# A selective scan on one core: which engine makes the products with B, how far ahead, and when a block's output is written back

## The chip, the cores and the metric

The kernel runs on one core of a Trainium2 chip. The metric is the device time of one execution in microseconds (us). A core has five engines that run at the same time, each with its own queue of instructions in a fixed order: TensorE (PE in the profile, its weight loads PEld), VectorE (DVE), ScalarE (ACT), GpSimd (POOL) and SyncE (SP), which here issues the DMA transfers. Engines wait for one another by semaphores. SBUF is the working memory, PSUM holds the results of TensorE.

## The reference

The program is a chain of four layers on an input of 2 x 128 x 64 x 64 fp32. Layers 0 to 2 are untouched. The change is in layer 3, a state-space layer: the normalised image is scanned in four directions, each scan is a Mamba block with 256 inner channels and 16 states per channel, and the four outputs are fused and added to the input.

```python
xz = x @ W_in.T
xh, z = jnp.split(xz, 2, axis=-1)
...
xh = jax.nn.silu(xc).transpose(0, 2, 1)          # xc: causal convolution of 4 taps
x_dbl = xh @ W_xp.T                               # -> dt, Bm, Cm
dt = jax.nn.softplus(dt @ W_dt.T + b_dt)
A = -jnp.exp(A_log)
dA = jnp.exp(dt[..., None] * A)                   # the decays
dBu = dt[..., None] * Bm[:, :, None, :] * xh[..., None]   # the products with B
def step(h, inp):
    dA_t, dBu_t = inp
    h = dA_t * h + dBu_t
    return (h, h)
_, hs = lax.scan(step, h0, (dA.transpose(1, 0, 2, 3), dBu.transpose(1, 0, 2, 3)))
y = jnp.einsum('lbdn,bln->bld', hs, Cm)           # multiplication with C, sum over states
y = y + xh * Dp
y = y * jax.nn.silu(z)
return y @ W_out.T
```

## The kernel before

**Tiling.** Layer 3 works through 64 blocks: 2 images, 4 directions, 8 blocks of 512 positions each. The 256 inner channels are two halves (`hf` 0 and 1) of 128. The 16 states are four groups of four (`ng` 0 to 3). A *group* is one (block, `hf`, `ng`): 128 channels by 4 states by 512 positions, so a block has eight groups, in the order `hf` 0 with `ng` 0 to 3, then `hf` 1 with `ng` 0 to 3. The 512 rows of a group are laid out as four *quarters* of 128 partitions (32 channels by 4 states), so that a group's tile `db` is 128 x 4 x 512.

**What happens to a group k.** `weights(k)` (L1384) spreads B over the partitions by a matmul into the PSUM tile `pbc` (pool `psb`, two buffers). `db_dve(k)` (L1400) multiplies it on VectorE with the spread input, for the first n quarters, into `db`; `db_pool(k)` (L1408) does the other 4 - n on GpSimd, from a copy `b4` of B that DMAs have spread over the partitions (`copies`, L1391)[...]. `expo` (L1417) makes the decays of one quarter on ScalarE into a PSUM tile `da` (three buffers). `scan` (L1423) is the recurrence of one quarter on VectorE; it overwrites `db`. `keep` (L1431, ScalarE) copies the last state for the next block, `cmul` (L1436, GpSimd) multiplies the whole `db` with C in place, and `sums` (L1441, TensorE) adds up the states into the PSUM tile `py`. After that the `db` buffer is free again; the pool `l3wk` has four. The table `ND[hf][ng]` (L1130) is n, the quarters that VectorE makes.

**What happens once a block.** `gate` (VectorE) multiplies with silu(z); `project` (L1458, TensorE) adds the projection to the image so far; `finish` (L1468, ScalarE) copies this PSUM tile back into the image, or in the last direction to the output. The next block is prepared at the same time: `conv`, `xproj`, `delta`, `sum_parts` and others (TensorE), silu, softplus and copies (ScalarE), `spread` (L1364, GpSimd), and a round trip through DRAM that spreads the inputs over partitions (`spread_store`, `spread_load` on SP).

**What sets the order.** Every engine's queue is written out by hand under `manual_schedule`. The main loop (L1600) goes over k, one group at a time; `slot` is k modulo 8. In the turn of group k it issues: the transfers of this slot; `weights(k + 2)`; `finish` of the block before where slot is 6; then for each quarter q an `expo` two quarters ahead and the `scan` of (k, q), with `keep(k - 1)` after the first `expo` and a `gate` after q = 1 in slots 2 and 6; then `db_dve(k + 1)`, `db_pool(k + 1)`, `cmul(k - 1)`, the preparation of the next block for this slot (`front_pe`, `front_act`, `front_pool`: two `spread` in slots 3 and 4, softplus in slots 1 and 2, silu with its table loads in slots 4 and 7), and `sums(k - 2)`. In slot 5 `sums(k - 2)` comes first and is followed by `project` and the next block's first `conv`. `psm`, the PSUM pool that `project` and the convolutions share, has two buffers. In eight blocks (22 to 29 of the loop's count) the layer norm of the second image is done beside the rest: `ln_mean`, `ln_less` after the scans of slot 0, `ln_var` and `ln_log` in slot 3, `ln_root`, `ln_scale` (GpSimd, slot 4).

The lines of the loop around the change:

```python
                if slot == 6 and 1 <= i <= NBK:
                    finish(i - 1)
                for q in range(4):
                    ...
                    if 4 * k + q + AHEAD < len(units):
                        expo(*units[4 * k + q + AHEAD])
                    ...
                    if live:
                        scan(k, q)
                ...
                if more:
                    db_dve(k + 1)
                    db_pool(k + 1)
                if ended:
                    cmul(k - 1)
```

Of the kernel before, what the change touches and what calls it, by code (L numbers as in the profile page):

```python
# [10 lines left out]
F32 = mybir.dt.float32  # L11
# [1109 lines left out]
def layer3(g, I, out):  # L1121
# [5 lines left out]
    nc, tc = g.nc, g.tc  # L1127
    NJ = 4

    ND = ((4, 2, 1, 4), (1, 4, 1, 4))  # L1130
    NNG = N_STATE // NJ
    HB = 1
    HC = 3
    with ExitStack() as ctx:
# [39 lines left out]
                    nc.tensor.transpose(pw[:, s * P : (s + 1) * P], ws, g.ident)  # L1174
                nc.vector.tensor_copy(wcs[:, hf].rearrange("p s o -> p (s o)"), pw)
        d4 = ctx.enter_context(tc.tile_pool(name="l3d4", bufs=2))
        wk = ctx.enter_context(tc.tile_pool(name="l3wk", bufs=4))
        up = ctx.enter_context(tc.tile_pool(name="l3u", bufs=2))
        ck = ctx.enter_context(tc.tile_pool(name="l3ck", bufs=2))

# [203 lines left out]
        def weights(k):  # L1384

            i, hf, ng = groups[k]
            pb = psb.tile([P, BLK], F32, name="pbc")
            nc.tensor.matmul(pb, sel[:, ng].rearrange("p j c -> p (j c)"), S[i]["bc"], start=True, stop=True)  # L1388
            G[k] = {"pb": pb}

        def copies(i, x, ng):  # L1391

            if x == "b" and ND[0][ng] == ND[1][ng] == 4:
                return
            t = S[i][x, ng] = ck.tile([P, BLK], F32, name=f"{x}4_{ng}", bufs=1)
            r0 = NJ * ng + (N_STATE if x == "c" else 0)
            for j in range(NJ):
                nc.sync.dma_start(t[32 * j : 32 * j + 32], S[i]["bx"][r0 + j].partition_broadcast(32))

        def db_dve(k):  # L1400
            i, hf, ng = groups[k]
            x, n = G[k], ND[hf][ng]
            x["db"] = wk.tile([P, 4, BLK], F32, name="db")
            nc.vector.tensor_tensor(  # L1404
                x["db"][:, :n, :], x.pop("pb").unsqueeze(1).to_broadcast([P, n, BLK]), S[i]["d4", hf][:, 1, :n, :], ALU.mult
            )

        def db_pool(k):  # L1408
            i, hf, ng = groups[k]
            x, n = G[k], ND[hf][ng]  # L1410
            if n == 4:
                return
            nc.gpsimd.tensor_tensor(  # L1413
                x["db"][:, n:, :], S[i]["b", ng].unsqueeze(1).to_broadcast([P, 4 - n, BLK]), S[i]["d4", hf][:, 1, n:, :], ALU.mult
            )

        def expo(k, q):  # L1417
            i, hf, ng = groups[k]
# [17 lines left out]
        def cmul(k):  # L1436
            i, hf, ng = groups[k]
            v = G[k]["db"]
            nc.gpsimd.tensor_mul(v, v, S[i]["c", ng].unsqueeze(1).to_broadcast([P, 4, BLK]))  # L1439
# [28 lines left out]
        def finish(i):  # L1468
            b, nd, c = blocks[i]
            s_ = S.pop(i)  # L1470
            if nd == 0:
                nc.scalar.activation(s_["xv"], img(s_["pf"]), AF.Identity, bias=vec(g, "b_fuse"))
            elif nd < 3:
                nc.scalar.copy(s_["xv"], img(s_["pf"]))
            else:
                res = ck.tile([P, BLK], F32, name="res", bufs=1)
                nc.scalar.copy(res, s_["pf"])
                nc.sync.dma_start(out[b, :, c * BLK : (c + 1) * BLK], res)
# [29 lines left out]
        def transfers(i, slot):  # L1508
            if i < NBK:
                if slot == 1:  # L1510
                    bc_store(i)
                elif slot == 4:
                    spread_store(i, 0)
                elif slot == 5:
                    spread_load(i, 0)
                    spread_store(i, 1)
            if slot == 0 and i - 1 < NBK:
                spread_load(i - 1, 1)
            for x, ahead in (("b", 3), ("c", 1)):
                j, ng = divmod(8 * (i - 1) + slot + ahead, 8)  # L1520
                if ng < NNG and 0 < j < NBK:
                    copies(j, x, ng)
# [32 lines left out]
        with tc.manual_schedule():  # L1555
            tc.keep_in_program_order(nc.scalar.preload_act_table_set("natural_log_exp_and_others"))
            nc.scalar.activation(am, am, AF.Exp)
            nc.vector.tensor_scalar(am, am, -1.0, None, ALU.mult)
            nc.vector.memset(xt[:, :HC], 0.0)
            nc.vector.memset(xt[:, HC + L :], 0.0)  # L1560
            nc.vector.memset(xn[:, HB - 1, HW - HC :], 0.0)
            nc.vector.memset(xn[:, HB + HW, :HC], 0.0)

            for t in range(NBLK + 2):
                slot = t - 2
                if slot == 6:
                    for k in range(2):
                        weights(k)
                    db_dve(0)
                    db_pool(0)  # L1570
                if slot >= 0:
                    front_pe(0, slot)
                    front_act(0, slot)
                    front_pool(0, slot)
                if slot == 1:
                    bc_store(0)
                elif slot in (3, 4):
                    spread_store(0, slot - 3)
                    if slot == 3:
                        spread_load(0, 0)  # L1580
                        copies(0, "b", 0)
                        copies(0, "c", 0)
                if t < NBLK:
                    for part in (ln_mean, ln_less, ln_square):
                        part(0, t)
                if 0 <= t - 1 < NBLK:
                    for part in (ln_var, ln_log, ln_root, ln_scale, ln_store):
                        part(0, t - 1)
                if t == 1:
                    begin(0)  # L1590
                    conv(0, 1)
                    conv_silu(0)
            for ng in range(1, NNG):
                copies(0, "b", ng)
                copies(0, "c", ng)
            units = [(k, q) for k in range(len(groups)) for q in range(4)]
            AHEAD = 2
            for u in range(AHEAD):
                expo(*units[u])
            for k in range(len(groups) + 7):  # L1600
                i, slot = divmod(k, 8)
                live = k < len(groups)
                more = k + 1 < len(groups)
                ended = 1 <= k <= len(groups)
                transfers(i + 1, slot)
                if k + 2 < len(groups):
                    weights(k + 2)
                norm = next_norm(i)
                if slot == 6 and 1 <= i <= NBK:
                    finish(i - 1)  # L1610
                for q in range(4):
                    if norm and slot == 3 and q == 3:
                        ln_log(*norm)
                    if 4 * k + q + AHEAD < len(units):
                        expo(*units[4 * k + q + AHEAD])
                    if norm and q == 0:
                        if slot == 0:
                            ln_mean(*norm)
                        elif slot == 3:
                            ln_var(*norm)  # L1620
                    if q == 0 and ended:
                        keep(k - 1)
                    if live:
                        scan(k, q)

                    for j, hf in (((k - 6) // 8, 0), ((k - 10) // 8, 1)):
                        if q == 1 and 8 * j + 6 + 4 * hf == k and 0 <= j < NBK:
                            gate(j, hf)
                if norm and slot == 0:
                    ln_less(*norm)  # L1630
                if more:
                    db_dve(k + 1)
                    db_pool(k + 1)
                if ended:
                    cmul(k - 1)

                if slot == 5 and 0 <= k - 2 < len(groups):
                    sums(k - 2)
                if slot == 5 and 1 <= i <= NBK:
                    project(i - 1)  # L1640
                front_pe(i + 1, slot)
                front_act(i + 1, slot)
                front_pool(i + 1, slot)
                if norm:
                    if slot == 1:
                        ln_square(*norm)
                    elif slot == 3:
                        ln_root(*norm)
                    elif slot == 4:
                        ln_scale(*norm)  # L1650
                    elif slot == 6:
                        ln_store(*norm)
                if live:

                    if slot == 6 and i % (4 * NBLK) < NBLK // 2:
                        for n in range(2):
                            turn(blocks[i][0], 2 * (i % (4 * NBLK)) + n)

                if slot != 5 and 0 <= k - 2 < len(groups):
                    sums(k - 2)  # L1660
# [160 lines left out]
```

## Time and profile before

| | us |
|---|---|
| median of 3 runs | 5898.72 (5897.96 to 5899.47) |
| profiled execution, its time | 5899.89 |
| profiled execution, its span | 5898.1 |
| layer 3's scans, first to last in the trace | 2523 to 5884 |
| busy in the whole span: DVE, POOL | 4452.2, 3632.0 |
| busy in the whole span: PE, ACT | 4930.2, 3816.1 |

The profile's page gives, for the whole span, how long each engine was busy, the same in 40 equal slices with a digit for tenths, and the costliest groups of instructions: line, engine, operation, the tile written and the tiles read, their shapes, the count, the busy time and the mean duration in ns, and behind the last bar the idle time of the engine just before these instructions with what ended it. The layers 0 to 2 take the first 2450 us; shares over the whole span therefore say little on layer 3, and the views are best asked for its stretch alone. A timeline line has the start, the time, the engine, the line and operation, the tiles, the count of merged instructions, and in brackets an idle time ahead of it with the instruction that ended it. A waits line has who waited for whom, the total, the number of times and the longest.

### The profile page before, as it was taken

Reading aid. Unit: us, or ns where it says so; the run is one execution under the profiler, and the core shown is the slowest. Engines: PE = TensorE matmul, PEld = TensorE weight load, DVE = VectorE, ACT = ScalarE, POOL = GpSimd, SP = SyncE. Lnnn points to the kernel's source line nnn. Section 1 sums busy time; section 2 is a strip of 40 time slices with the busy share of each in tenths; the row PEclk is TensorE's granted clock in tenths of the full one; section 3 lists DMA queues with packets and bytes.
Section 4 is the critical chain, followed back from the end, with each engine's and each line's share of the span. In section 5 each row is a group of like instructions: output and inputs, shape, how many; then the busy total and the mean of one; then the engine's idle time right before and its main releaser. Section 6 shows DMA issues by size and latency. Waiting matters only on the chain.

```text
span 5898.1 us, 58825 instructions
## 1 busy us (share of the span) xinstructions
PE 4930.2 (84%) x19238; PEld 1735.4 (29%) x19238; DVE 4452.2 (75%) x4266; ACT 3816.1 (65%) x5499; POOL 3632.0 (62%) x1200
## 2 busy tenths in 40 slices
PE   7999999989978779877777787878777787777776
PEld 3333333334434334322222222222222222222221
DVE  5333333355124688589999999999999999999998
ACT  4888888840035511377777777777777777777775
POOL 5111111100010021089999999999999999999999
PEclk8999999999988889988888888888888888888887
DMA  5000001030056200056655556555655566555564
GB/s 155 19 19 19 19 19 33 1 59 1 4 112 109 64 11 0 20 131 146 143 133 135 130 140 145 128 131 141 151 134 134 129 139 146 139 132 134 137 148 104
DMA packets 345402, 558.75 MB, mean 95 GB/s; under 512 B 70480, under 2 KB 125280, under 8 KB 344000
## 3 DMA queue, kind: packets, MB, share of 16 engines
q1 hardware_dynamic: 341952, 551.37, 40.4%
q10 hardware_dynamic: 3136, 3.56, 0.2%
q8 instruction: 152, 2.49, 0.2%
q14 instruction: 162, 1.33, 0.1%
HBM read 465.59 MB, written 89.13 MB: 94 GB/s over the span
## 4 chain that ended last, share of the span: by engine, by line
PE 52%; DVE 27%; POOL 9%; issue 5%; DMA 4%; ACT 2%; SPq 1%; DVEq 0%; POOLq 0%; ACTq 0%
DVE db L1429 18%; PE ps L287 10%; PE acc L303 8%; DVE db L1404 7%; POOL db L1439 6%; PE pm L1294 6%; PE m L1052 6%; PE m L566 5%; PE py L1447 2%; PE pm L1359 2%; PE pm L1466 2%; PE pm L1464 2%; PE acd L812 2%; DMA dx<-dd 1%; POOL dd L1367 1%
## 5 line engine op out<-in xcount | busy, mean ns | idle before, releaser
L1439 POOL TENSOR_TENSOR db<-db,c 128x2048 f32<-128x2048 f32 x512 | 2313.4, 4535 | 92.3 <-ACT hl L1434 82.6
L1429 DVE TENSOR_TENSOR_SCAN db<-da,hl,db 128x512 f32<-128x512 f32 x1792 | 2166.1, 1266 | 69.1 <-ACT da L1420 21.1
L1420 ACT ACTIVATE da<-dd,am 128x512 f32<-128x512 f32 x2048 | 1398.0, 689 | 727.5 <-DVE db L1429 701.2
L293 ACT ACTIVATE e<-ps 128x1024 f16<-128x1024 f32 x1024 | 992.2, 1021 | 135.6 <-PE ps L287 123.9
L1388 PE MATMUL pbc<-bc,sel 64*128 64x512 f32 x512 | 288.3, 563 | 695.4 <-DVE db L1404 695.3
L1413 POOL TENSOR_TENSOR db<-b,dd 128x1536 f32<-128x1536 f32 (+1 forms) x256 | 811.5, 3170 | 9.0 <-PE py L1447 4.4
L1404 DVE TENSOR_TENSOR db<-pbc,dd 128x2048 f32<-128x2048 f32 (+2 forms) x512 | 785.3, 1534 | 0.6 <-PE pbc L1388 0.6
L314 DVE RECIPROCAL rec<-acc 32x512 f32<-32x512 f32 x64 | 214.9, 3358 | 640.4 <-PE acc L303 640.4
L321 POOL TENSOR_TENSOR parts<-parts 32x512 f32<-32x512 f32 x64 | 80.5, 1257 | 976.2 <-DVE parts L320 976.2
L1447 PE MATMUL py<-db,fold 128*32 128x512 f32 x4096 | 639.7, 701 | 39.8 <-POOL db L1439 38.4
L287 PE MATMUL ps<-q,k 32*128 32x512 f32 x4096 | 656.4, 643 | 3.6 <-DVE flag L250 2.8
L303 PE MATMUL acc<-e,v 128*128 128x512 f16 x2048 | 532.1, 382 | 0.0
L1388 PEld LDWEIGHTS pbc<-bc,sel 64*128 64x128 f32 x512 | 105.8, 207 | 1184.1 <-DVE db L1404 1070.4
L1052 PE MATMUL m<-v,u 128*128 128x512 f32 x864 | 379.7, 603 | 49.3 <-DVE v L1021 49.3
L1359 PE MATMUL pm<-dd,ident 128*128 128x512 f32 x512 | 365.3, 852 | 4.6 <-ACT dd L1352 4.4
L1429 DVE TENSOR_TENSOR_SCAN db<-da,db 128x512 f32<-128x512 f32 x256 | 294.8, 1206 | 30.4 <-ACT da L1420 22.5
L303 PEld LDWEIGHTS <-v 128*128 128x128 bf16 x2048 | 158.5, 97 | 510.6 <-issue 389.4
L287 PEld LDWEIGHTS ps<-q,k 32*128 32x128 f32 x4096 | 229.4, 184 | 228.4 <-issue 169.6
L566 PE MATMUL m<-comb,w 64*128 64x512 f32 (+4 forms) x1296 | 269.9, 575 | 0.0
L686 POOL TENSOR_SCALAR yt<-y 32x512 f32<-32x512 f32 x8 | 18.2, 2272 | 379.8 <-DVE y L677 379.4
L1052 PEld LDWEIGHTS m<-v,u 128*128 128x128 f32 x864 | 166.9, 194 | 262.1 <-issue 216.1
L1294 PE MATMUL pm<-xn,wcs 128*128 128x512 f32 x512 | 237.1, 606 | 3.0 <-ACT z L1312 2.6
(317 smaller groups left out, 5991.2 us busy)
## 6 DMA issues: line engine op xcount, KB each, us to landing
dd<-dx SPq DMA_DIRECT2D x1024, 256.0 KB, 6.8
dx<-dd SPq DMA_DIRECT2D x128, 512.0 KB, 3.3
c<-bx SPq DMA_DIRECT2D x1024, 64.0 KB, 2.2
b<-bx SPq DMA_DIRECT2D x768, 64.0 KB, 3.3
hats<-pos SPq DMA_DIRECT2D x136, 256.0 KB, 9.8
q<-qd SPq DMA_DIRECT2D x32, 512.0 KB, 7.5
w<-in_conv0T SPq DMA_DIRECT2D x18, 288.0 KB, 8.8
q<-in_x SPq DMA_DIRECT2D x8, 512.0 KB, 6.3
```

The lines of the kernel that those rows point to most:

```text
L287: nc.tensor.matmul(ps[:, i, :], k4[h % 2][rows, kb // 4, :], q4[h % 2][rows, qb * BLK : (qb + 1) * BLK], start=True, stop=True,)
L293: nc.scalar.activation(e[:, :n, :], ps[:, :n, :], AF.Exp)
L303: nc.tensor.matmul(acc, v3[b][:, kb, h, :], e[:, i, :], start=(kb == 0), stop=(kb == NS - 1))
L566: yield lambda q=q, dy=dy, src=src, i0=i0, i1=i1: nc.tensor.matmul(m[:, i0 * NF : i1 * NF], w[half, dy, q, x, :], src, start=(dy == KC and ...
L1052: nc.tensor.matmul(m[x], weights[j][:, dy, x, :], v[j][b][:, x, r0 : r0 + RP, :].rearrange("p r i -> p (r i)"), start=(dy == 0), stop=(dy ...
L1294: nc.tensor.matmul(pu, wcs[:, hf, s, :], window(blk, sgn * s), start=(s == 0), stop=(s == 3))
L1404: nc.vector.tensor_tensor(x["db"][:, :n, :], x.pop("pb").unsqueeze(1).to_broadcast([P, n, BLK]), S[i]["d4", hf][:, 1, :n, :], ALU.mult)
L1413: nc.gpsimd.tensor_tensor(x["db"][:, n:, :], S[i]["b", ng].unsqueeze(1).to_broadcast([P, 4 - n, BLK]), S[i]["d4", hf][:, 1, n:, :], ALU.mult)
L1420: nc.scalar.activation(da, S[i]["d4", hf][:, 0, q, :], AF.Exp, scale=am[:, hf, q, ng : ng + 1])
L1429: nc.vector.tensor_tensor_scan(d1, d0, d1, 0.0 if first else hl[:, hf, ng, q, :], ALU.mult, ALU.add)
L1439: nc.gpsimd.tensor_mul(v, v, S[i]["c", ng].unsqueeze(1).to_broadcast([P, 4, BLK]))
L1447: nc.tensor.matmul(S[i]["y", hf][32 * q : 32 * q + 32, :], fold, G[k]["db"][:, q, :], start=False, stop=(ng == NNG - 1),)
```

## The change

It alters which engine makes which products, the time at which GpSimd makes them, the number of `db` buffers, and the place of `finish`:

- `ND` changes from ((4, 2, 1, 4), (1, 4, 1, 4)) to ((4, 0, 1, 4), (4, 4, 0, 4)). VectorE still makes 21 of a block's 32 quarters. GpSimd makes all four quarters of two groups (`hf` 0 `ng` 1, `hf` 1 `ng` 2) and three of a third (`hf` 0 `ng` 2). Groups with n = 0 get no matmul in `weights` and no VectorE product; for `ng` 0 no copy of B is loaded any more.
- `db_pool` is called two groups ahead (for k + 2, after `cmul(k - 1)`) instead of one (for k + 1, before `cmul(k - 1)`); the copies of B start one group earlier; the pool `l3wk` has five buffers.
- `finish` of the block before moves within the turn of slot 6 from ahead of all four `expo` to ahead of the last.

```diff
-    ND = ((4, 2, 1, 4), (1, 4, 1, 4))
+    ND = ((4, 0, 1, 4), (4, 4, 0, 4))
...
-        wk = ctx.enter_context(tc.tile_pool(name="l3wk", bufs=4))
+        wk = ctx.enter_context(tc.tile_pool(name="l3wk", bufs=5))
...
         def weights(k):
             i, hf, ng = groups[k]
+            G[k] = {}
+            if ND[hf][ng] == 0:
+                return
             pb = psb.tile([P, BLK], F32, name="pbc")
             nc.tensor.matmul(pb, sel[:, ng].rearrange("p j c -> p (j c)"), S[i]["bc"], start=True, stop=True)
-            G[k] = {"pb": pb}
+            G[k]["pb"] = pb
...
+        def db_tile(k):
+            if "db" not in G[k]:
+                G[k]["db"] = wk.tile([P, 4, BLK], F32, name="db")
+            return G[k]["db"]
...
         def db_dve(k):
             i, hf, ng = groups[k]
-            x, n = G[k], ND[hf][ng]
-            x["db"] = wk.tile([P, 4, BLK], F32, name="db")
-            nc.vector.tensor_tensor(
-                x["db"][:, :n, :], x.pop("pb").unsqueeze(1).to_broadcast([P, n, BLK]), S[i]["d4", hf][:, 1, :n, :], ALU.mult
-            )
+            n = ND[hf][ng]
+            if n:
+                nc.vector.tensor_tensor(
+                    db_tile(k)[:, :n, :], G[k].pop("pb").unsqueeze(1).to_broadcast([P, n, BLK]),
+                    S[i]["d4", hf][:, 1, :n, :], ALU.mult,
+                )
...
-            for x, ahead in (("b", 3), ("c", 1)):
+            for x, ahead in (("b", 4), ("c", 1)):
...
+            db_pool(1)
             units = [(k, q) for k in range(len(groups)) for q in range(4)]
...
-                if slot == 6 and 1 <= i <= NBK:
-                    finish(i - 1)
                 for q in range(4):
+                    if slot == 6 and q == 3 and 1 <= i <= NBK:
+                        finish(i - 1)
...
                 if more:
                     db_dve(k + 1)
-                    db_pool(k + 1)
                 if ended:
                     cmul(k - 1)
+                if k + 2 < len(groups):
+                    db_pool(k + 2)
```

`db_pool` takes its tile from `db_tile` too; its arithmetic stays.

More of the change, by code (lines that the diff above doesn't have):

```diff
@@ L1398, in copies @@
                 nc.sync.dma_start(t[32 * j : 32 * j + 32], S[i]["bx"][r0 + j].partition_broadcast(32))
+        def db_tile(k):
+            if "db" not in G[k]:
+                G[k]["db"] = wk.tile([P, 4, BLK], F32, name="db")
+            return G[k]["db"]
         def db_dve(k):
             i, hf, ng = groups[k]
-            x, n = G[k], ND[hf][ng]
-            x["db"] = wk.tile([P, 4, BLK], F32, name="db")
-            nc.vector.tensor_tensor(
-                x["db"][:, :n, :], x.pop("pb").unsqueeze(1).to_broadcast([P, n, BLK]), S[i]["d4", hf][:, 1, :n, :], ALU.mult
-            )
+            n = ND[hf][ng]
[4 more added lines that the diff above has]
+                )
         def db_pool(k):
             i, hf, ng = groups[k]
[L1410 to L1415, printed above, removed]
+            n = ND[hf][ng]
+            if n < 4:
+                nc.gpsimd.tensor_tensor(
+                    db_tile(k)[:, n:, :], S[i]["b", ng].unsqueeze(1).to_broadcast([P, 4 - n, BLK]),
+                    S[i]["d4", hf][:, 1, n:, :], ALU.mult,
+                )
         def expo(k, q):
```

## The prediction

> Within one of the 64 blocks I number the eight groups 0 to 7 (0 to 3 are `hf` 0, 4 to 7 are `hf` 1) and call step s the turn of the main loop whose four scans belong to group s. "Slot" in the code is this s.
>
> **What bounds the kernel now.** First the two busy rows of the page's 40 slices, then its costliest groups.
>
> ```profile
> DVE  5333333355124688589999999999999999999998
> POOL 5111111100010021089999999999999999999999
> ...
> L1439 POOL TENSOR_TENSOR db<-db,c 128x2048 f32<-128x2048 f32 x512 | 2313.4, 4535 | 92.3 <-ACT hl L1434 82.6
> L1429 DVE TENSOR_TENSOR_SCAN db<-da,hl,db 128x512 f32<-128x512 f32 x1792 | 2166.1, 1266 | 69.1 <-ACT da L1420 21.1
> ```
>
> From about 2520 us to the end VectorE and GpSimd are both full: two engines are close to being the bound, and which one it is must be read from a single block. The groups of that stretch, shapes kept apart, give the products with B on both engines:
>
> ```profile
> L1404 DVE TENSOR_TENSOR db<-pbc,dd 128x2048 f32<-128x2048 f32 x255 | 578.1, 2267 | 0.0
> L1404 DVE TENSOR_TENSOR db<-pbc,dd 128x512 f32<-128x512 f32 x192 | 128.0, 666 | 0.0
> L1404 DVE TENSOR_TENSOR db<-pbc,dd 128x1024 f32<-128x1024 f32 x64 | 76.9, 1202 | 0.0
> ...
> L1413 POOL TENSOR_TENSOR db<-b,dd 128x1536 f32<-128x1536 f32 x192 | 660.5, 3440 | 9.0 <-PE py L1447 4.4 <-DMA c<-bx 3.0 <-POOL db L1439 0.9
> ...
> L1413 POOL TENSOR_TENSOR db<-b,dd 128x1024 f32<-128x1024 f32 x63 | 148.6, 2359 | 0.0
> ```
>
> Durations overlap or leave gaps, so the price of an instruction is read from start to start, in VectorE's timeline of a quiet block:
>
> ```profile
> 3153.59 1.20 DVE L1404 TENSOR_TENSOR db<-pbc,dd 128x1024 f32<-128x1024 f32 x1
> 3154.89 4.81 DVE L1429 TENSOR_TENSOR_SCAN db<-da,hl,db 128x512 f32<-128x512 f32 x4
> 3159.61 0.67 DVE L1404 TENSOR_TENSOR db<-pbc,dd 128x512 f32<-128x512 f32 x1
> 3160.38 2.46 DVE L1429 TENSOR_TENSOR_SCAN db<-da,hl,db 128x512 f32<-128x512 f32 x2
> ...
> 3178.29 2.27 DVE L1404 TENSOR_TENSOR db<-pbc,dd 128x2048 f32<-128x2048 f32 x1
> 3180.66 4.81 DVE L1429 TENSOR_TENSOR_SCAN db<-da,hl,db 128x512 f32<-128x512 f32 x4
> ```
>
> Four scans take 4.72 (3154.89 to 3159.61); a product of 1, 2 or 4 quarters takes 0.77, 1.30 or 2.37. A gate takes 0.58. Block: 8 x 4.72 + 4 x 2.37 + 1.30 + 3 x 0.77 + 2 x 0.58 = 52.0. The gates of quiet blocks lie 52.08 apart, so **VectorE sets the pace** there with no wait at all. GpSimd, the same way: 8 multiplications with C at 4.49, three 3.39, one 2.35, two `spread` at 1.24: 50.9. Over 64 blocks some time comes on top; the waits of VectorE (2600 to 5880 us), ScalarE and GpSimd (2523 to 5898 us), in us in total, times, longest:
>
> ```profile
> DVE db L1429 <- ACT da L1420: 33.1, 29, 3.2
> ...
> ACT xa L1474 <- PE pm L1466: 85.1, 32, 4.9
> ...
> POOL db L1439 <- ACT hl L1434: 82.6, 59, 5.7
> ```
>
> Listing every start in VectorE's timeline against its usual spacing (which also finds the short ones) puts the scans' waits in two places: before scans 2 and 3 of group 6, 23.7 us in 34 cases; before scan 3 of group 4 in the eight blocks that carry the second image's layer norm, 14.5 us. Their causes, from TensorE's and ScalarE's timelines:
>
> ```profile
> 3180.61 0.49 PE L1388 MATMUL pbc<-bc,sel 64*128 64x512 f32 x1 [3.68 <-DVE db L1404]
> ...
> 3187.08 1.12 ACT L1474 COPY xa<-pm 128x512 f32<-128x512 f32 x1 [2.06 <-PE pm L1466]
> ...
> 3755.51 0.57 ACT L1340 CAST bc<-pm 32x512 fp32r<-32x512 f32 x1 [1.59 <-PE pm L1337]
> ```
>
> In step 5 TensorE stands 3.68 us at `weights`, whose PSUM buffer VectorE frees late; `project` is queued behind it, `finish` on ScalarE waits for `project`, and the decays of group 6 are queued behind `finish`.
>
> [...] scans hold 1266 ns with GpSimd full. [...] from the trace 0.24 us (0.77 less a quarter's 0.53).
>
> **The change, part by part.**
> 1. *Products on VectorE.* The quarters stay 21 of 32, in six instructions instead of eight: 5 x 2.37 + 0.77 = 12.62 against 13.09. Saved 0.47 a block, **30 us** in 64; all of it on the path, since VectorE never idles in a quiet block. New pace 51.6.
> 2. *Products on GpSimd.* Four quarters: no such row; 3.39 + (3.39 - 2.35) = 4.43, and the equal-shaped multiplication with C takes 4.49. I take 4.45. 2 x 4.45 + 3.39 = 12.29 against 12.52: 50.7 a block. Slack 0.9.
> 3. *Order and arrival.* Moving `db_pool` behind `cmul` and one group further ahead leaves those two in the same order on GpSimd's queue; only `spread` falls one place back. I walk its queue with step 0 at 0. VectorE's steps start at 0, 4.7, 10.2, 17.9, 25.0, 32.1, 36.8, 44.5. ScalarE copies group 7's state (`keep`) behind the silu of the next block, so `cmul` 7 starts at 2.0 (read: 3150.90 against 3148.86). Product 2: 6.5 to 9.9, needed from scan 2 of group 2 on, at 11.4: 1.5 to spare. `cmul` 0 and 1 to 18.8, `cmul` 2, `spread`, `cmul` 3 to 29.4, product 6 to 33.9, needed at 36.8: 2.9 to spare. `spread` to 35.1, `cmul` 4 to 6 to 48.6, product 1 to 53.0, needed at 56.3: 3.3 to spare. So nothing on VectorE waits; cost 0, from 0 to +26 (below).
> 4. *Queues passed.* The second `spread` ends at 35.1 after step 4 begins at 25.0, about as late as now, so its store on SP too. Copies of B follow that store: eight of up to 0.9 us issue, done near 43, landed near 46, needed at 48.6 and 53. Four DMA issues a block vanish (group 0 needs no copy). Cost 0, SP being ahead.
> 5. *`weights`.* Two matmuls a block go. The one of step 5 now reuses a buffer freed in step 3, so the 3.68 goes, and the wait behind it is for `cmul` 3 (29.4). `sums` and `project` take 6 us more: 35.5, before `finish` is reached.
> 6. *`finish` later.* It reaches ScalarE at 39.9, three decays later, and ends at 41; the decay behind it still waits for a scan ending then. The 23.7 go; I leave 1: **-23**. Behind `finish` wait, on TensorE, the second convolution (its PSUM buffer) and `sums` 4: done at about 46.2. GpSimd wants the tile of `sums` 4 for product 1 at 48.6 (the fifth tile makes it this one): 2.4 to spare.
> 7. *Eight layer-norm blocks.* After step 3 VectorE now has a product of 2.37 instead of 0.77, so the wait at group 4 shrinks by 1.6 each: 14.5 to 3.7, **-11**. After step 0 it has none instead of 1.30: ScalarE's copies of the projection (3734.50, held by TensorE) let the decay of scan 3 of group 1 be ready 8.5 after the step's start, and VectorE is there at 7.7: **+7** for eight blocks (0 to +10). In other blocks that decay is ready at 6.0, needed at 7.1.
> 8. *Fifth tile, start.* The first scan waits for ScalarE (10.5 us) while GpSimd makes product 1: 0.
>
> Sum: -30 - 23 - 11 + 7 = -57 from the profiled 5899.9 (span 5898.1, 1.8 around it; the median 5898.7 is 1.2 below): 5842.
>
> **Rivals.**
> - *GpSimd paces.* It has 0.9 us in 52; if its waits for `keep` take more than that where work is due, VectorE's 0.47 returns as a wait. For: it is 98% full. Against: it is ahead at every need above. Gain of the waits alone, 34 less 3: 5869.
> - *The first quarter waits for the others.* If VectorE's quarter of group 2 is held until GpSimd's three are written (9.9 against 9.4), 0.4 x 64 = 26: 5868. Against: GpSimd now writes its share before VectorE begins, without a wait shown.
> - *Slower: the tile comes late.* `finish`, TensorE's convolution, `sums` 4, product 1, in that chain: if GpSimd stands y us a block for the tile, 0.9 are free and the rest goes to VectorE. From y = 1.8 the gain is lost; at 2.7 it is +115 - 57: 5958. It needs `sums` 4 over 4 us later than I walk it.
> - *No effect*, because waits fill every gap: 5899.
>
> **Numbers.** Likeliest case 0.70, at 5842, from 5830 (all 38 us of waits gone, none new) to 5855; GpSimd paces 0.12; first quarter 0.07; slower 0.08; none 0.03. To leave out no more than 2 in 10, the range goes from 5829 to 5874. A measurement tells about 0.2%, 12 us, from no change: faster 0.89, same 0.03, slower 0.08.
>
> **What would show it.** VectorE's products in two shapes, 5 and 1 a block; GpSimd's full ones near 4.53 us; gates 51.6 apart in quiet blocks; ScalarE's wait before L1474's copy almost gone; VectorE's waits for decays under 15 us. Wrong if VectorE waits for GpSimd's `db` in most blocks, or if GpSimd waits for `py` (tile release) for over 1 us a block.

## The result, and the profile after

The changed kernel takes 5844.64 us (median of 4 runs, 5840.38 to 5847.68) against 5899.1: a ratio of 0.9907, 95% interval 0.989 to 0.9925. The profiled execution took 5845.92 us, with a span of 5844.1. In the changed file the scans stand at L1438, VectorE's products at L1412, GpSimd's at L1421, the multiplication with C at L1448, `keep` at L1443, `finish` at L1481 to L1486.

The groups of the layer-3 stretch (2500 to 5846 us), shapes kept apart, VectorE's rows and then GpSimd's:

```profile
L1412 DVE TENSOR_TENSOR db<-pbc,dd 128x2048 f32<-128x2048 f32 x320 | 724.8, 2265 | 0.6 <-PE pbc L1391 0.6
...
L1412 DVE TENSOR_TENSOR db<-pbc,dd 128x512 f32<-128x512 f32 x64 | 42.6, 665 | 0.0
...
L1448 POOL TENSOR_TENSOR db<-db,c 128x2048 f32<-128x2048 f32 x512 | 2309.6, 4530 | 57.1 <-ACT hl L1443 52.0 <-DMA dd<-dx 3.1 <-DMA c<-bx 0.7
L1421 POOL TENSOR_TENSOR db<-b,dd 128x2048 f32<-128x2048 f32 x128 | 578.8, 4522 | 0.0
L1421 POOL TENSOR_TENSOR db<-b,dd 128x1536 f32<-128x1536 f32 x64 | 220.3, 3442 | 0.0
```

VectorE makes five full products and one of a quarter per block, and GpSimd's full product costs what a multiplication with C costs. VectorE's timeline of a quiet block:

```profile
3187.14 2.26 DVE L1412 TENSOR_TENSOR db<-pbc,dd 128x2048 f32<-128x2048 f32 x1
3189.51 9.51 DVE L1438 TENSOR_TENSOR_SCAN db<-da,hl,db 128x512 f32<-128x512 f32 x8
3198.93 0.67 DVE L1412 TENSOR_TENSOR db<-pbc,dd 128x512 f32<-128x512 f32 x1
```

Eight scans now run through without a product between them; the next product starts 9.42 after the first scan, 1.18 for each scan. Gates of quiet blocks lie 51.56 apart instead of 52.08. The waits of VectorE and GpSimd (2600 to 5830 us):

```profile
DVE db L1438 <- ACT da L1429: 11.3, 14, 1.6
DVE db L1438 <- POOL db L1421: 3.7, 5, 1.1
...
POOL db L1448 <- ACT hl L1443: 45.9, 48, 4.5
```

VectorE's 33.1 us behind decays became 11.3. In step 5 of that quiet block TensorE no longer stands at `weights`, and `finish` finds its input ready (TensorE's lines, then ScalarE's copy, which has no bracket):

```profile
3218.69 1.06 PE L1456 MATMUL py<-db,fold 128*32 128x512 f32 x8 [2.44 <-POOL db L1448]
3220.81 2.26 PE L1473 MATMUL pm<-xa,ident 128*128 128x512 f32 x2 [1.05 <-ACT z L1312]
...
3229.40 1.12 ACT L1483 COPY xa<-pm 128x512 f32<-128x512 f32 x1
```

Listing every start in VectorE's timeline as before: the waits at group 6 are gone (0.1 us); what stays is some 18 us, 15.5 of it at three places in and around the eight layer-norm blocks: 2.1 us before scan 3 of group 1, 7.3 before scan 2 of group 2, 6.1 before scan 3 of group 4. The account: 0.52 x 64 = 33 from the pace and about 22 from waits (39.8 to some 18) give 55; the spans differ by 54.0.

### The profile page after: what moved, and what is told of

It is laid out like the page before. It is cut to its first block, busy times and chain, and to the rows that moved or that the text cites. A ratio compares the mean times of both kernels' runs of the same rounds, so it can differ in the third digit from the quotient of the medians.

```text
span 5844.1 us, 57551 instructions
## 1 busy us (share of the span) xinstructions
PE 4898.7 (84%) x19110; PEld 1732.8 (30%) x19110; DVE 4430.6 (76%) x4138; ACT 3829.3 (66%) x5499; POOL 3621.2 (62%) x1136
## 4 chain that ended last, share of the span: by engine, by line
DVE 50%; PE 37%; issue 5%; POOL 3%; DMA 2%; ACT 2%; SPq 1%; DVEq 0%; POOLq 0%; ACTq 0%
DVE db L1438 36%; DVE db L1412 12%; PE ps L287 11%; PE acc L303 9%; PE m L1052 6%; PE m L566 5%; PE acd L812 2%; DVE gt L1465 1%; PE m L526 1%; POOL db L1448 1%; PE pf L775 1%; POOL db L1421 1%; PE pc L663 1%; DMA hats<-pos 1%; SPq L748 1%
## 5 line engine op out<-in xcount | busy, mean ns | idle before, releaser
L1448 POOL TENSOR_TENSOR db<-db,c 128x2048 f32<-128x2048 f32 x512 | 2309.6, 4530 | 57.1 <-ACT hl L1443 52.0
L1438 DVE TENSOR_TENSOR_SCAN db<-da,hl,db 128x512 f32<-128x512 f32 x1792 | 2155.0, 1263 | 47.6 <-ACT da L1429 9.5
L1456 PE MATMUL py<-db,fold 128*32 128x512 f32 x4096 | 618.1, 689 | 234.8 <-POOL db L1448 231.9
L1421 POOL TENSOR_TENSOR db<-b,dd 128x2048 f32<-128x2048 f32 (+1 forms) x192 | 799.1, 4162 | 0.0
L1412 DVE TENSOR_TENSOR db<-pbc,dd 128x2048 f32<-128x2048 f32 (+1 forms) x384 | 767.3, 1998 | 0.6 <-PE pbc L1391 0.6
L1391 PE MATMUL pbc<-bc,sel 64*128 64x512 f32 x384 | 209.8, 546 | 162.8 <-DVE db L1412 162.6
L1318 PE MATMUL pm<-u,wxp 128*72 128x512 f32 x256 | 197.6, 917 | 175.0 <-ACT u L1299 175.0
L1438 DVE TENSOR_TENSOR_SCAN db<-da,db 128x512 f32<-128x512 f32 x256 | 292.5, 1204 | 18.7 <-ACT da L1429 12.1
L1456 PEld LDWEIGHTS py<-db,fold 128*32 128x32 f32 x4096 | 90.4, 114 | 623.8 <-POOL db L1448 364.9
```

The lines of the kernel that those rows point to most:

```text
L1412: nc.vector.tensor_tensor(db_tile(k)[:, :n, :], G[k].pop("pb").unsqueeze(1).to_broadcast([P, n, BLK]), S[i]["d4", hf][:, 1, :n, :], ALU.mult,)
L1421: nc.gpsimd.tensor_tensor(db_tile(k)[:, n:, :], S[i]["b", ng].unsqueeze(1).to_broadcast([P, 4 - n, BLK]), S[i]["d4", hf][:, 1, n:, :], ALU ...
L1438: nc.vector.tensor_tensor_scan(d1, d0, d1, 0.0 if first else hl[:, hf, ng, q, :], ALU.mult, ALU.add)
L1456: nc.tensor.matmul(S[i]["y", hf][32 * q : 32 * q + 32, :], fold, G[k]["db"][:, q, :], start=False, stop=(ng == NNG - 1),)
```

## The experiments

Times are medians in us, ratios are to the kernel before in the same session; runs of different sessions are compared by their ratios. Lines are those of the changed kernel's numbering where nothing else is said.

### The parts alone

**The table alone** (`nd_only`): from the changed kernel, back to four tiles, B copies three ahead, no `db_pool(1)` ahead of the loop, `finish` in the old place, and

```diff
                     db_dve(k + 1)
+                    db_pool(k + 1)
                 if ended:
                     cmul(k - 1)
-                if k + 2 < len(groups):
-                    db_pool(k + 2)
```

> Only the table of products is new; GpSimd works one group ahead, four tiles, finish in its old place. Theory (the table alone is the cause): VectorE's products in six instructions, 0.47 x 64 = -30; weights of step 5 no longer holds TensorE, so project is done before finish is reached even in the old place, -20 to -23; layer-norm blocks about -1: 5842 to 5850, quiet blocks 51.6 apart. Rival (lead and fifth tile are needed): scans of the groups made whole by GpSimd wait for it, a line VectorE scan <- POOL product of over 30 us in total, 5870 to 5900.

Measured 5858.85, 0.9931 (0.9918 to 0.9945), 9 us over the theory's range. Quiet blocks are 51.6 apart and group 6's third scan never waits: the table gives the pace and takes the wait for `finish` away by itself. But group 6 has a new wait, at its first scan, 18.1 us in the eight layer-norm blocks. Its waits line, and one such place in GpSimd's and VectorE's timelines:

```profile
DVE db L1438 <- POOL db L1421: 17.4, 8, 2.5
```

```profile
3744.15 1.27 POOL L1367 TENSOR_TENSOR dd<-dd,u 128x512 f32<-128x512 f32 x1
3745.38 1.26 POOL L1243 TENSOR_TENSOR xc<-xc,sq 128x512 f32<-128x512 f32 x1
3746.61 4.53 POOL L1421 TENSOR_TENSOR db<-b,dd 128x2048 f32<-128x2048 f32 x1
...
3751.17 2.46 DVE L1438 TENSOR_TENSOR_SCAN db<-da,hl,db 128x512 f32<-128x512 f32 x2 [2.13 <-POOL db L1421]
```

Product 6 stands behind the second `spread` and `ln_scale`, 2.5 us together, and the scan waits until it ends.

**The table alone, `ln_scale` later** (`nd_scale`): in the kernel above

```diff
-                    elif slot == 4:
+                    elif slot == 5:
                         ln_scale(*norm)
```

> The kernel with only the new table of products, and ln_scale of the layer norm moved from slot 4 to slot 5 on GpSimd, behind product 6 and cmul 4. Theory (the lead of two groups matters only because it puts product 6 ahead of ln_scale and of a spread in the eight layer-norm blocks): the 18 us that VectorE waits ahead of group 6 fall to 8 or less, 5843 to 5850. Rival (the lead does something else): 5855 to 5860 as with the table alone.

5847.81, 0.9918 (0.9904 to 0.9931), within the theory's range. The wait at group 6 fell from 18.1 to 7.2. So most of what the lead of two groups brings is product 6's place on GpSimd's queue, ahead of `ln_scale`, in those eight blocks.

**`finish` alone** (`fin_only`): the kernel before with

```diff
-                if slot == 6 and 1 <= i <= NBK:
-                    finish(i - 1)
                 for q in range(4):
+                    if slot == 6 and q == 3 and 1 <= i <= NBK:
+                        finish(i - 1)
```

> Only finish moves, all else as before. Theory: the waits of group 6 (23.7 us) vanish and nothing else changes: 5874 to 5878, quiet blocks stay 52.08 apart, the waits at group 4 of the layer-norm blocks stay at 14 us. Rival (finish late holds TensorE's second convolution and with four tiles the product of VectorE): 5890 to 5910.

5881.4, 0.9969 (0.9957 to 0.998), some 5 us less gain than expected, between the two ranges. The waits at group 6 fell from 23.7 to 2.8 and those at group 4 stayed at 14.5; the span fell by 18.5.

**All but `finish`** (`fin_undone`): the changed kernel with the reverse of that diff.

> The changed kernel with finish back ahead of group 6's decays. Theory (two causes that cover each other: with step 5's weights free, project ends at about the moment finish is reached in the old place): 5843 to 5850, ScalarE waits under 30 us for project in total, VectorE under 5 us at group 6. Rival (the place of finish is what removed the 23 us): 5865 to 5870.

5848.51, 0.9914 (0.99 to 0.9927): not to be told from the changed kernel. ScalarE waits 17 us for `project` in all (9.8, 5.6 and 1.8 in its three kinds of copy), VectorE 0.2 at group 6. The new table removes the wait by itself here, the later `finish` in `fin_only`; together they don't remove it twice.

**All but the table** (`nd_old4`): the changed kernel with four tiles and

```diff
-    ND = ((4, 0, 1, 4), (4, 4, 0, 4))
+    ND = ((4, 2, 1, 4), (1, 4, 1, 4))
```

> The changed kernel with the old table of products, and four tiles[...]. Theory: VectorE is back at eight product instructions, +0.47 x 64 = 30, quiet blocks 52.08 apart; the waits at group 6 stay away because finish is late: 5872 to 5880. Rival (the earlier products of GpSimd carry the gain): 5845 to 5855.

5878.98, 0.9964 (0.995 to 0.9977), within the theory's range: quiet blocks 52.1 apart, waits at group 6 1.0 us. Without the table the pace is the old one.

**All but the fifth tile** (`four_tiles`): in the changed kernel

```diff
-        wk = ctx.enter_context(tc.tile_pool(name="l3wk", bufs=5))
+        wk = ctx.enter_context(tc.tile_pool(name="l3wk", bufs=4))
```

> The changed kernel with four tiles for the products instead of five. Theory: the tile that a product of GpSimd needs is then that of sums two groups back, still done 2 us or more before GpSimd reaches the product, so 5843 to 5848 and no wait of GpSimd for py over 5 us in total. Rival (the fifth tile carries the lead): GpSimd waits 1 us or more a block for py, quiet blocks over 52, 5870 or more.

5845.1, 0.9905 (0.989 to 0.992), within the theory's range, and no wait of GpSimd for `py`: the fifth tile is worth nothing in this kernel.

### The slower rival's chain

`finish_late`: in the changed kernel

```diff
-                    if slot == 6 and q == 3 and 1 <= i <= NBK:
+                    if (slot, q) == ((7, 1) if i < NBK else (6, 3)) and 1 <= i <= NBK:
                         finish(i - 1)
```

> The changed kernel with finish moved on by 5.9 us, to ahead of the third decay issued in step 7. It prices the slower rival's chain: finish (45.8 to 46.9), second convolution (to 50.6), sums 4 (to 52.0), product 1 (to 56.5, needed at 56.3), cmul 7 (to 61.0), product 2 (to 64.4, needed at 63.0). Theory: VectorE waits about 1.4 us a block for product 2, quiet blocks 53.0 apart, 5920 to 5945, GpSimd waits 3 us a block for py. Rival (GpSimd has room for it, or the convolution is not what holds the tile): 5845 to 5860.

5920.91, 1.0035 (1.0021 to 1.0049): slower than before the change. VectorE's waits, then GpSimd's (2600 to 5825 us):

```profile
DVE db L1438 <- POOL db L1421: 48.4, 56, 1.4
DVE db L1438 <- ACT da L1429: 29.8, 37, 2.1
...
POOL db L1421 <- issue: 53.2, 29, 4.2
POOL db L1421 <- DVE db L1412: 34.6, 15, 2.8
POOL db L1421 <- DVE db L1438: 19.2, 7, 4.0
```

By the listing VectorE waits 56.3 us in 61 blocks ahead of the second scan of group 2, 0.92 a block where 1.4 was expected, and 27.8 for the decay of group 0's third scan, which was not expected. GpSimd stands 111 us ahead of product 1 (the three lines and two smaller ones), in 53 blocks, 1.8 a block on average. The waits view names no releaser that was still busy; TensorE's and GpSimd's timelines show it:

```profile
3143.68 5.28 PE L1294 MATMUL pm<-xt,wcs 128*128 128x512 f32 x8 [3.84 <-ACT xa L1483]
3149.75 1.93 PE L1456 MATMUL py<-db,fold 128*32 128x512 f32 x16
...
3150.98 4.54 POOL L1421 TENSOR_TENSOR db<-b,dd 128x2048 f32<-128x2048 f32 x1 [1.75 <-issue]
```

The second convolution starts when `finish` ends, `sums` 4 (the first eight of the sixteen) comes behind it, and in all 53 blocks product 1 starts 0.17 us after the last matmul of `sums` 4 has ended. So the chain is the one expected. Its sizes are not. The edit moves `finish` by less than the expectation says: it stands ahead of the second decay issued in step 7, not the third, and starts (medians) 10.9 us after step 5 begins instead of 7.8, which is 3.0 later and not 5.9. `sums` 4 ends 4.6 later, because the convolution took 5.4 us there and 3.7 in the changed kernel; why is left open. The decays come late by the same chain: ScalarE's silu of the next block, which reads that convolution, waits 43.3 us for TensorE in 34 cases, and the decay of group 0's third scan is queued behind it. That the time came out at the edge of the expected range is therefore in part luck. 1.8 less the free 0.9 is close to VectorE's 0.92, but only on average: where GpSimd stands 2.7 and 1.5 in turn, VectorE waits 1.2 and 0.8.

### What the 0.24 us of an instruction is

**Two halves** (`split`): `db_dve` makes the products of `ng` 3 in two instructions.

```diff
+                for a, b in ((0, 2), (2, 4)) if ng == 3 else ((0, n),):
+                    nc.vector.tensor_tensor(
+                        db_tile(k)[:, a:b, :], pb.unsqueeze(1).to_broadcast([P, b - a, BLK]),
+                        S[i]["d4", hf][:, 1, a:b, :], ALU.mult,
+                    )
```

> The changed kernel with the four-quarter products of the two groups with ng = 3 each made in two instructions of two quarters, one behind the other: 8 product instructions a block again, same elements. Theory A (each instruction has its price of 0.24 us, wherever it stands): +0.47 x 64 = 30, 5873 to 5877. Theory B (0.19 of the 0.24 is the scan standing still until the product in front of it is written, and only 0.05 is the instruction): +0.11 x 64 = 7 or less, 5843 to 5853.

5828.45, 0.9885 (0.9869 to 0.99), below both ranges: two more instructions a block, and by the ratios some 13 us *less* than the changed kernel. Quiet blocks are 51.29 apart instead of 51.56, which is 17 us in 64. VectorE's timeline (in this file the products stand at L1414, the scans at L1440):

```profile
3202.70 2.33 DVE L1414 TENSOR_TENSOR db<-pbc,dd 128x1024 f32<-128x1024 f32 x2
3204.95 4.80 DVE L1440 TENSOR_TENSOR_SCAN db<-da,hl,db 128x512 f32<-128x512 f32 x4
```

The scan starts 80 ns before the second half ends, instead of 104 ns after a whole product: it reads the first half, which by the mean of 1204 ns for a half had ended some 1.05 us before. Theory A falls; B was right in kind and still too careful, as it left the gap standing.

**The product ahead of the last scan** (`early_product`): in the changed kernel

```diff
+                    if q == 3 and more:
+                        db_dve(k + 1)
                     if live:
                         scan(k, q)
...
-                if more:
-                    db_dve(k + 1)
```

> The changed kernel with VectorE's product for the next group issued ahead of the last scan of the group before, so that the scan behind a product does not read it. Theory B: the gap of +104 ns behind each of six products a block becomes an overlap of -83 ns as between scans, VectorE's pace falls to 51.56 - 6 x 0.187 = 50.4 and GpSimd's 50.7 becomes the bound: quiet blocks 50.7 to 51.2, 5790 to 5822. Theory A: no change, 5842 to 5849.

5805.79, 0.9845 (0.9832 to 0.9859), within Theory B's range. VectorE's timeline:

```profile
3163.23 2.26 DVE L1412 TENSOR_TENSOR db<-pbc,dd 128x2048 f32<-128x2048 f32 x1
3165.41 8.32 DVE L1438 TENSOR_TENSOR_SCAN db<-da,hl,db 128x512 f32<-128x512 f32 x7
...
3197.23 1.28 DVE L1438 TENSOR_TENSOR_SCAN db<-da,hl,db 128x512 f32<-128x512 f32 x1 [0.28 <-POOL db L1421]
```

Where the scan behind a product has nothing else to wait for, the gap is now an overlap of 79 ns. Quiet blocks are 50.7 to 50.8 apart, which is GpSimd's own sum, and VectorE waits for GpSimd in nearly every block (74 times, 40.1 us, against 5 times and 3.7): the bound has moved.

### The eight layer-norm blocks

**Layer norm later** (`norm_later`): in the changed kernel, and with `ln_var` and `ln_log` in slot 5 instead of 3 within the loop over q,

```diff
-                    if slot == 1:
+                    if slot == 2:
                         ln_square(*norm)
-                    elif slot == 3:
+                    elif slot == 5:
                         ln_root(*norm)
-                    elif slot == 4:
                         ln_scale(*norm)
```

> The changed kernel with the second image's layer norm spread otherwise: ln_square in slot 2 instead of 1, ln_var, ln_log, ln_root and ln_scale in slot 5 instead of 3 and 4. Theory: the 15 us that VectorE still waits in eight blocks come from the ScalarE and TensorE work put into steps 1 and 3, where the next product is short or TensorE's chain is long; moved to places with cover, 10 to 13 us go: 5831 to 5836. Rival (GpSimd's 1.27 more in those blocks is what makes it late): the waits stay, 5842 to 5848.

5834.84, 0.9888 (0.9872 to 0.9903), within the theory's range. GpSimd does the same work in these blocks and the waits at groups 2 and 4 are gone, so its 1.27 alone was not their cause. A wait of 6.8 us is new, before the first gate.

**With more gate buffers** (`norm_gates`): the same, with four product tiles instead of five and

```diff
-            gt = s_["gt", hf] = ck.tile([P, BLK], F32, name="gt")
+            gt = s_["gt", hf] = ck.tile([P, BLK], F32, name="gt", bufs=4)
```

> The later layer norm with four buffers for the gates' output instead of two, and four product tiles to make room. Theory (the 6.8 us that the first gate waits there are for project of the block before, which reads the buffer that this gate writes): they go, 5826 to 5830. Rival (the gate waits for its own sums): 5833 to 5837.

5836.72, 0.9898 (0.9883 to 0.9913): no gain, which is the rival's time but not for its reason. The gate's wait is gone, as the theory had it, but 8.9 us appeared before VectorE's first product of the next block, in the same eight blocks. It is the missing fifth tile: with four tiles that product takes the tile of `sums` 4, which TensorE reaches late there, and in seven of the eight blocks it starts 0.12 us after the last matmul of `sums` 4 has ended. In `norm_later`, with five tiles, it starts before `sums` 4 ends in all eight, without a wait.

**Early product and later layer norm** (`combined`): the diffs of `early_product` and `norm_later` on the changed kernel, with its five tiles.

> The early product and the later layer norm together, five tiles, two gate buffers. Theory: outside the eight layer-norm blocks GpSimd sets the pace at 50.7 as with the early product alone; in those eight GpSimd needs 51.95, so of the 53 that they take now about 1 each can go: 5795 to 5803. Rival (in those blocks TensorE's delayed project and sums become the next wait, as in the later layer norm alone): no gain over the early product, 5803 to 5810.

5797.53, 0.9827 (0.9813 to 0.9841), within the theory's range and the fastest kernel here. Its waits (2600 to 5780 us):

```profile
DVE db L1438 <- POOL db L1421: 28.2, 63, 1.3
DVE gt L1465 <- PE pm L1475: 6.4, 6, 1.5
...
POOL db L1448 <- ACT hl L1443: 2.0, 2, 1.1
```

GpSimd practically never waits: it paces layer 3.

## Why the prediction was right, point by point

The sum was -57 us and the spans differ by 54.0. That is closer than its terms are: the pace gave 33 for 30, the layer-norm blocks gained nothing (15.5 us of waits after, 14.5 before) where 4 were expected, and the two misses partly cancel. That part is luck.

1. *Products on VectorE.* The count, the sign and the price held, 0.52 a block measured for 0.47 (the rest is about 1.5 ns on each of the 32 scans); without the table (`nd_old4`) it is lost. **The reason given was wrong.** The prediction laid the saving to the count of instructions, at 0.24 us each. The traces do show a fixed part, 0.13 us in the duration (666 ns for one quarter, 533 for each further one), but 0.08 of it is hidden under the neighbour, and 0.05 is left. Most of the 0.24 is a scan that reads what the instruction in front of it has just written; 0.187 of it (104 + 83 ns) goes when the order changes. `split` adds instructions and gains. Each product that the table saved took its hand-over with it, so the price was right for this change; taken as a price per instruction it gives `split` the wrong sign and `early_product` no gain. What the 0.187 consists of, these runs don't separate.
2. *Products on GpSimd.* 4.45 start to start was taken, the timelines give 4.49; the rows give a duration of 4.522, that of the multiplication with C (4.530) less 8 ns.
3. *Order and arrival.* In quiet blocks nothing waits for GpSimd, as walked: products 2, 6 and 1 have 1.4, 3.1 and 3.2 us to spare (medians), for 1.5, 2.9 and 3.3. The walk was made for quiet blocks alone. In the layer-norm blocks product 6 has 0.3 us or less to spare in six of eight, and in and just behind them product 2 has nothing in seven cases; without the lead (`nd_only`) group 6 waits 18 us for product 6.
4. *Queues passed.* No wait on a copy of B appears on VectorE, and 0.7 us on GpSimd for a copy of C. Right.
5. and 6. *`weights`, `finish`.* The 23 went, but the two steps are one: either alone removes it (all but 2.8 us in `fin_only`). The chain through the second convolution holds, with a margin near the one walked (2.4 us; in the changed kernel product 1 starts a median of 2.1 after `sums` 4 ends in quiet blocks): in `finish_late` `sums` 4 is 4.6 later, and 76 us are lost.
7. *Layer-norm blocks.* **The term that was mis-sized:** 10.7 us of waits were left, 15.5 were measured. Group 1's is 2.1 for 7, group 4's 6.1 for 3.7, and group 2's 7.3 was not in the sum. There ScalarE's copy `bc` waits for TensorE, the decay and `keep` behind it are late, and GpSimd stands (its timeline, then ScalarE's, of one such block):

```profile
3787.51 1.26 POOL L1367 TENSOR_TENSOR dd<-dd,u 128x512 f32<-128x512 f32 x1
3791.37 4.54 POOL L1448 TENSOR_TENSOR db<-db,c 128x2048 f32<-128x2048 f32 x1 [2.59 <-ACT hl L1443]
...
3789.36 0.57 ACT L1340 CAST bc<-pm 32x512 fp32r<-32x512 f32 x1 [1.59 <-PE pm L1337]
...
3791.11 0.18 ACT L1443 COPY hl<-db 128x4 f32<-128x4 f32 x1
```

   `cmul` 3 starts 0.08 us after `keep` 3 ends, product 6 ends just before its scan wants it, and with 1.27 of `ln_scale` on top product 2 is a microsecond late. The waits view puts several of these on ScalarE; the timelines show the scan starting 0.03 us after product 2 ends, seven times, when its decay had been ready for over 3 us.
8. *Fifth tile, start.* The tile is worth nothing in this kernel (`four_tiles`), though a later layer norm uses it (`norm_gates`). The start is unchanged.

Of the rivals, "GpSimd paces" was not true of this change but is of `early_product`; "the first quarter waits" never showed; "the tile comes late" was true of `finish_late` only (in `norm_gates` it is a product of VectorE that waits for its tile).

## What to carry to other kernels

Price an instruction from start to start, but ask what the price is: a gap behind it that turns into an overlap when the next instruction reads something else (104 ns after the product here, 79 before its end in `early_product`) is a hand-over, not a cost of the instruction. Here the reordering of `early_product` was then worth more a block than the merging (0.8 us for 0.52). Where two edits remove the same wait, undo each alone before giving it to either. And walk the rare blocks as well as the common ones: product 2's margin, a median of 1.4 us in quiet blocks, was gone in seven blocks in and just behind the layer norm.

## What the runs showed that was not expected

On VectorE a scan behind a product that it does not read started 79 ns before that product's recorded end (`early_product`; 80 in `split`), and behind a product that it reads 104 ns after it (the kernels before and after the change). GpSimd at work all the time did not stretch VectorE's scans: in the changed kernel 1715 scans with GpSimd busy throughout took 1263 ns on average and the seven with GpSimd idle throughout 1262; in `early_product`, which GpSimd paces, scans took 1259.
